# Two graph layers on one core: softmax weights turned by VectorE instead of TensorE, row sums from a column of ones, values evicted whole, and several loads and stores queued elsewhere

## The chip, the cores and the metric

The kernel runs on one core of a Trainium2 chip. The metric is the device time of one execution in microseconds (us), as the median of several runs. Engines are named as in the profile: PE is TensorE, DVE is VectorE, ACT is ScalarE, POOL is GpSimd, and SP is the engine that only issues transfers.

## The reference

Input x has 128 graphs of 64 nodes with 768 features, all float32, and adj is a 0/1 matrix of 64x64 for each graph. Two layers follow each other, both with a residual and a layer norm.

```python
# layer 0, per graph: attention of h with itself, masked and renormalised
p = softmax(h @ h.T / sqrt(768)); delta = p * adj
attn = delta / (delta.sum(2) + 1e-10)
ctx = upper(attn) @ (h @ W_left.T + b_left) + diag(attn) * (h @ W_self.T + b_self) \
    + lower(attn) @ (h @ W_right.T + b_right)
x = layernorm(h + relu(layernorm_affine(ctx)))
# layer 1, per graph: 12 heads of 64
q, k, v = (x @ W + b for W in (Wq, Wk, Wv))          # split into heads
s = where(adj > 0, q @ k.T / 8 + beta * adj, -9e15)
x = layernorm(x + softmax(s) @ v)
```

## The kernel before

**Tiling.** The 8192 tokens are cut into 16 blocks of 512 tokens (8 graphs). A tile of 128 tokens (T = 4 of them in a block) holds two graphs, g = 0 and 1, one in each half of the partitions. Layer 0 of block m = n+1 is worked on beside layer 1 of block n. All arithmetic is float32.

**The big products.** Six weight matrices, s (self), l (left), r (right), v, q and k, are applied by `seven()` with seven products of half size in place of eight (Strassen-like). It runs 14 groups of matmuls, numbered 0 to 13 here: for each of the seven factors in the order 1, 2, 6, 5, 7, 4, 3 one group for j = 0 and one for j = 1. Two PSUM tiles X and two Y (tags "X" and "Y", `ps_st`) take the sums; `first()` copies an intermediate sum out and `last()` writes a result. An accumulation goes on in the same X after `first()` has read it, so the next group that adds to this X waits for that read. For s, l, r and v (`by_tokens`) each group is three products with 384 columns; for q and k (`projected`, one call for each of three head groups hg) it is three with 256 columns, and there `first()` runs on ACT.

**The pieces of the weights.** [...] `prepare()` forms the seven factors at the start and stores those that are new to DRAM; after that every stage streams its seven pieces of 576 KB through the four buffers of `wst`, on SP's queue. The q and k pieces are stored by POOL's queue in `qk_d`.

**The order of work.** From the main loop on, the order is as written. Stages follow each other: `left` (side_part l of block m), `right` (side_part r), `own` (self_part), `val` (values of block n), `qk[0]`, `qk[1]`, `qk[2]` (projected). Hooks are callables that a stage runs before group number `place`; `at(left, 11, sides, m)` puts `sides` before group 11 of `left`. Small work waits in two queues, `urgent` and `lazy`, from which `step()` takes one item after each group; items marked `act` (work for ACT) and GAP let the lazy queue have its turn as well, and `settle(key)` runs everything that a later part needs at once. Hooks of n = 1 to 14 carry layer 1 of the block before, p = n-1.

**Layer 1's attention.** `scores(n, hg)` makes 32 small products into two PSUM tiles, scales and masks them on DVE and queues max, subtraction, exponential (one ACT instruction of 128x1024), sum, reciprocal and multiplication (all 128x1024 on DVE). `turned_weights` turns the result with 8 PE transposes of 128x128 into PSUM tiles `ps_e` and copies them back with two ACT copies to `eT`. `weighted` multiplies with v into `ps_y`, and `added` adds that to x. Head group 0 is scored in `qk[1]` and weighted in `qk[2]`, head group 1 is scored in `qk[2]` and weighted in the next block's `left`, head group 2 is scored and weighted in `left`.

**Values.** Rows of v must lie in the half of the partitions that their product with eT reads, so `last()` in `values` writes each 128x384 result with four DVE instructions of 64x192, which also move between the halves.

**The last block** has nothing beside its layer 1; its attention is done at the end, for two tiles at a time.

Of the kernel before, what the change touches and what calls it, by code (L numbers as in the profile page):

```python
# [11 lines left out]
F32 = mybir.dt.float32  # L12
# [32 lines left out]
def gnn_two_layers(ctx: ExitStack, tc, x, adj, wl, bl, ws, bs, wr, br, gamma, beta,  # L45
# [14 lines left out]
    ps_tr = ctx.enter_context(tc.tile_pool(name="ps_tr", bufs=2, space=PSUM))  # L60
    ps_mm = ctx.enter_context(tc.tile_pool(name="ps_mm", bufs=2, space=PSUM))
# [68 lines left out]
    def settle(key):  # L130

        for queue in (urgent, lazy):
            while any(item[0] == key for item in queue):
                queue.popleft()[1]()
# [3 lines left out]
    pieces = {}  # L138
# [5 lines left out]
    def prepare(nm, quarter_pool, sum_pool, waits=(0, 0, 0)):  # L144

        w = weights[nm].rearrange("(p c) e -> p c e", c=KC)
        src = {(0, 0): w[:, 0:HC, 0:HALF], (0, 1): w[:, 0:HC, HALF:D],
               (1, 0): w[:, HC:KC, 0:HALF], (1, 1): w[:, HC:KC, HALF:D]}  # L150
        b = {}
        for q in ((0, 0), (1, 0), (0, 1), (1, 1)):
            b[q] = quarter_pool.tile([P, HC, HALF], F32, tag="w", name=f"b{q[0]}{q[1]}_{nm}")
            nc.sync.dma_start(out=b[q], in_=src[q])
        t5, t6, t4 = (sum_pool.tile([P, HC, HALF], F32, tag="w", name=f"t{i}_{nm}") for i in (5, 6, 4))
        in_sbuf = {1: b[0, 0], 2: b[1, 0], 3: b[1, 1], 5: t5, 6: t6, 7: b[0, 1], 4: t4}
        key = ("w", nm)
        if nm in "slrv":
            d = tc.dram_tile([4, P, HC, HALF], F32, name=f"d_{nm}")
            pieces[nm] = {1: src[0, 0], 2: src[1, 0], 3: src[1, 1], 5: d[0], 6: d[1], 7: d[2], 4: d[3]}  # L160

        def store(i):
            if nm in "slrv":
                if i in (5, 6, 7, 4):
                    nc.gpsimd.dma_start(out=pieces[nm][i], in_=in_sbuf[i])
            else:

                with tc.issue_after(last_sum[1].ins):
                    for hg in range(NHG):
                        nc.gpsimd.dma_start(out=qk_d[hg, i - 1, :, "qk".index(nm)],  # L170
                                            in_=in_sbuf[i][:, :, hg * P : (hg + 1) * P])

        def formed(i, out, left, right):
            nc.vector.tensor_tensor(out, left, right, ALU.subtract)
            store(i)

        def idle():
            pass

        later(key, *[idle] * waits[0], partial(formed, 5, t5, b[0, 1], b[0, 0]),  # L180
              *[idle] * waits[1], partial(formed, 6, t6, b[1, 1], t5), partial(formed, 7, b[0, 1], b[1, 1], b[0, 1]),
              *[idle] * waits[2], partial(formed, 4, t4, b[1, 0], t6))
        if nm in "qk":
            later(key, lambda: store(1), lambda: store(2), lambda: store(3))
        return in_sbuf

    def transposed(src, xT, t):

        for c0 in range(0, KC, 3):
            ps = ps_tr.tile([P, 4, P], F32, tag="tr", name="ps_x")  # L190
            for c in range(3):
                nc.tensor.transpose(ps[:, c, :], src[:, c0 + c :: KC], ident)
            nc.scalar.copy(xT[:, c0 : c0 + 3, t * P : (t + 1) * P], ps[:, 0:3, :])
# [92 lines left out]
    def by_tokens(nm, S, last, in_sbuf=None, hooks={}):  # L286
# [3 lines left out]
        def factors(i, j):  # L290
            if i not in wt:
                wt[i] = wst.tile([P, HC, HALF], F32, tag="w", name=f"w{nm}")
                nc.sync.dma_start(out=wt[i], in_=pieces[nm][i])
            return [(S[i][:, k, j * P : (j + 1) * P], wt[i][:, k, :]) for k in range(HC)]
# [78 lines left out]
    def sides(n):  # L373
# [3 lines left out]
        aps = ps_tr.tile([P, T, P], F32, tag="tr", name="ps_a")  # L377
# [108 lines left out]
    def values(n, hooks={}):  # L486


        blk = blocks[n]
        v = l1_p.tile([P, T, 2, HP, HD], F32, tag="v", name=f"v_{n}")  # L490
        blk["v"] = v

        def last(t, h, ps, part):
            def pairs(a):
                return a.rearrange("p (j r d) -> p r j d", r=2, d=HD)

            add = pairs(bias["v"][:, h * HALF : (h + 1) * HALF] if part is None else part)
            for r in range(2):
                for g in range(2):
                    rows = slice(g * L, (g + 1) * L)  # L500
                    nc.vector.tensor_tensor(v[r * L : (r + 1) * L, t, g, h * 3 : (h + 1) * 3, :],  # L501
                                            pairs(ps)[rows, r], add[rows, r], ALU.add)

        by_tokens("v", blk["S"], last, None, hooks)
# [30 lines left out]
    def scores(n, hg, pool=None):  # L535

        blk = blocks[n]
        q, k = blk["qk"]

        s = (pool or l1s_p).tile([P, T, 2, 2, L], F32, tag="lr" if pool else "s", name="s")  # L540
# [13 lines left out]
        s8 = s.rearrange("p t c r m -> p (t c r) m")  # L554
        mx = st.tile([P, T * 4], F32, tag="mx1", name="mx1")
        z = st.tile([P, T * 4], F32, tag="z1", name="z1")
        rz = st.tile([P, T * 4], F32, tag="rz1", name="rz1")

        def per_row(v):
            return v[:, :, None].to_broadcast([P, T * 4, L])  # L560

        def sums():
            nc.vector.tensor_reduce(z, s8, AX.X, ALU.add)
            nc.vector.reciprocal(rz, z)

        later(("s", n, hg),
              lambda: nc.vector.tensor_tensor(s4, s4, add[:, :, None, :].to_broadcast([P, T, 4, L]), ALU.add),
              lambda: nc.vector.tensor_reduce(mx, s8, AX.X, ALU.max),
              lambda: nc.vector.tensor_tensor(s8, s8, per_row(mx), ALU.subtract),
              act(lambda: nc.scalar.activation(s8, s8, AF.Exp)), GAP, sums,  # L570
              lambda: nc.vector.tensor_tensor(s8, s8, per_row(rz), ALU.mult), queue=urgent)
        blk[hg] = s

    def turned_weights(n, hg, tiles=range(T), pool=None):

        blk = blocks[n]
        settle(("s", n, hg))
        e = blk[hg]
        if 0 in tiles:
            blk["eT", hg] = (pool or l1_p).tile([P, T, 2, P], F32, tag="lr" if pool else "eT", name="eT")  # L580
        eT = blk["eT", hg]
        for t0 in tiles[::2]:
            ps = ps_tr.tile([P, 4, P], F32, tag="tr", name="ps_e")
            for t in range(2):
                for c in range(2):
                    nc.tensor.transpose(ps[:, 2 * t + c, :], e[:, t0 + t, c].rearrange("p r m -> p (r m)"), ident)  # L586
            nc.scalar.copy(eT[:, t0 : t0 + 2].rearrange("p t c i -> p (t c) i"), ps)

    def weighted(n, hg, tiles=range(T)):

        blk = blocks[n]
        xt, v, eT = blk["x"], blk["v"], blk["eT", hg]
        y = [ps_mm.tile([P, T, 2, HD], F32, tag="mm", name=f"ps_y{r}") for r in range(2)]
        for t in tiles:
            for c in range(2):
                for r in range(2):
                    rows = slice(r * L, (r + 1) * L)
                    for g in range(2):
                        cols = slice(g * L, (g + 1) * L)
                        nc.tensor.matmul(y[r][cols, t, c, :], lhsT=eT[rows, t, c, cols],  # L600
                                         rhs=v[rows, t, g, hg + c * HC, :], start=True, stop=True)

        def added(t):
            res = xt[t].rearrange("p (c k r d) -> p r c k d", c=2, k=HC, r=2)
            for r in range(2):
                nc.vector.tensor_add(res[:, r, :, hg, :], res[:, r, :, hg, :], y[r][:, t])

        def both(ts):
            for t in ts:
                added(t)  # L610

        later(("y", n, hg), *[partial(both, tiles[i : i + 2]) for i in range(0, len(tiles), 2)], queue=urgent)
# [66 lines left out]
    l1s_p = ctx.enter_context(tc.tile_pool(name="l1s", bufs=2))  # L679
# [6 lines left out]
    for n in range(NBLK):  # L686
# [13 lines left out]
        if p >= 0:  # L700
            one, two, three = (left, left, right) if not last else (qk[0], qk[1], qk[1])
            at(one, 1 if not last else 2, scores, p, 2)
            at(one, 1 if not last else 2, turned_weights, p, 1)
            at(one, 5, weighted, p, 1)
            at(two, 11 if not last else 2, turned_weights, p, 2)
# [3 lines left out]
        if not last:  # L709
            if n > 0:  # L710
# [9 lines left out]
                at(right, 9, begin1)  # L720
# [5 lines left out]
                at(own, 0, begin2)  # L726
                for t in range(T):
                    at(own, t, lambda t=t: fetch["fs"][t]())
                for a in range(P // Q):
                    at(right, 9 + a, lambda a=a: sq1["fs"][a]())  # L730
# [48 lines left out]
        if not last:  # L779
            at(qk[2], 2, turned_weights, n, 0)  # L780
# [4 lines left out]
    values(n, {2: [partial(scores, n, 2, l0t)]})  # L785

    for t0 in (0, 2):
        for hg in range(NHG):
            turned_weights(n, hg, range(t0, t0 + 2), l0t if hg else None)
        for hg in range(NHG):  # L790
            weighted(n, hg, range(t0, t0 + 2))
            settle(("y", n, hg))
        finish(n, range(t0, t0 + 2))
# [32 lines left out]
```

## Time and profile before

| | |
|---|---|
| median of 3 runs | 3092.37 us (3086.59 to 3094.2) |
| span of the profiled execution | 3078.1 us |
| PE busy | 2983.9 us, 97% |
| DVE busy | 2227.8 us, 72% |
| ACT busy | 396.8 us, 13% |
| POOL busy | 354.3 us, 12% |
| data moved | 541.20 MB, mean 176 GB/s |

A row of the groups' table reads: line, engine, operation, output<-inputs, shapes, xcount, then busy us and mean ns of one, then idle time of the engine just before and what ended it. A row of the timeline reads: start, duration, engine, line, operation, count, and in brackets how long the engine had been idle and for whom it had waited. One product in float32 shows as two matmul records, so a group of three products is x6.

In the middle of the run the pattern repeats every block: `projected` for head group 0 starts at 1392.4 us in one block and at 1580.5 us in the next, 188.2 us later.

### The profile page before, as it was taken

How to read it: one execution, taken by the hardware profiler on the slowest of the kernel's cores; microseconds unless marked ns; L12 is line 12 of the kernel's file. 1: busy time of each engine (PE TensorE's matmuls, PEld its weight loads, DVE VectorE, ACT ScalarE, POOL GpSimd, SP SyncE). 2: the span in 40 equal slices, each digit the busy share in tenths (PEclk: the TensorE clock that was granted, in tenths of full speed). 3: DMA queues.
4: the chain of work that ended last, by engine and by line, in shares of the span. 5: the costliest groups of instructions: out<-in, count | busy, mean ns of one | idle time of the engine just before them, and what ended most of it. 6: DMA issues, size and time to landing. Idle time of an engine off the chain costs nothing.

```text
span 3078.1 us, 45049 instructions
## 1 busy us (share of the span) xinstructions
PE 2983.9 (97%) x18144; PEld 2015.0 (65%) x18144; DVE 2227.8 (72%) x4163; ACT 396.8 (13%) x691; POOL 354.3 (12%) x317
## 2 busy tenths in 40 slices
PE   8899999999999999999999999999999999999997
PEld 5457657576675766758567585665757667575685
DVE  5758767686776867768687686867768677686756
ACT  0101102021020200202011020110201102020031
POOL 2321010110101101011010111101011010110000
PEclk9999999999999999999999999999999999999998
DMA  8663655737557474574645756456573655746433
GB/s 284 211 230 121 190 174 166 216 118 217 152 161 213 124 229 139 161 215 145 212 139 162 211 160 208 132 179 191 161 221 119 215 156 162 220 127 220 128 123 119
DMA packets 261070, 541.20 MB, mean 176 GB/s; under 512 B 28576, under 2 KB 165408, under 8 KB 260864
## 3 DMA queue, kind: packets, MB, share of 16 engines
q1 hardware_dynamic: 185424, 429.38, 44.1%
q10 hardware_dynamic: 60848, 44.05, 7.2%
q0 software_dynamic: 14592, 64.89, 5.4%
q8 instruction: 145, 2.38, 0.3%
q14 instruction: 61, 0.50, 0.0%
HBM read 473.37 MB, written 64.88 MB: 175 GB/s over the span
## 4 chain that ended last, share of the span: by engine, by line
PE 77%; DVE 7%; issue 7%; DMA 7%; POOL 1%; ACT 0%; ACTq 0%; SPq 0%; POOLq 0%; DVEq 0%
PE ps_X L269 38%; PE ps_Y L269 30%; DMA ws<-in_L_gnn_W_self_dram 6%; DVE v L501 4%; PE ps_ctx L425 3%; DVE hT L211 2%; PE sc L548 1%; PE ps_y L600 1%; PE u L331 1%; PE ps_e L586 1%; DVE u L298 1%; DMA b_l<-in_L_gnn_W_left_dram 1%; DVE stats L239 0%; PE ps_a L379 0%; DMA d_v<-t_v 0%
## 5 line engine op out<-in xcount | busy, mean ns | idle before, releaser
L269 PE MATMUL ps_X<-xT,wqk 128*128 128x256 f32 x1728 | 388.8, 379 | 0.0
L269 PEld LDWEIGHTS ps_X<-xT,wqk 128*128 128x128 f32 x1728 | 328.2, 190 | 48.1 <-issue 0.4
L269 PE MATMUL ps_Y<-S,wqk 128*128 128x256 f32 x1152 | 264.3, 379 | 0.0
L410 DVE TENSOR_TENSOR lr<-ps_Y,u 64x384 f32<-64x384 f32 x384 | 213.2, 555 | 62.6 <-PE ps_Y L269 56.2
L522 ACT ACTIVATE uqk<-ps_X,bq 128x256 f32<-128x256 f32 x144 | 68.2, 474 | 1419.5 <-PE ps_X L269 1419.5
L269 PEld LDWEIGHTS ps_Y<-S,wqk 128*128 128x128 f32 x1152 | 218.9, 190 | 29.8
L269 PE MATMUL ps_X<-wv,xT 128*128 128x384 f32 x576 | 199.2, 492 | 0.3
L239 DVE BATCH_NORM_STATS2 stats<-o 128x6 f32<-128x384 f32 x384 | 192.4, 542 | 1.8
L269 PE MATMUL ps_X<-ws,hT 128*128 128x384 f32 x540 | 181.7, 491 | 7.4 <-DMA ws<-d_s 7.4
L269 PE MATMUL ps_X<-wl,hT 128*128 128x384 f32 x540 | 183.7, 486 | 0.0
L269 PE MATMUL ps_X<-wr,hT 128*128 128x384 f32 x540 | 179.1, 486 | 0.0
L501 DVE TENSOR_TENSOR v<-ps_Y,u 64x192 f32<-64x192 f32 x384 | 136.4, 355 | 41.7 <-PE ps_Y L269 35.6
L269 PE MATMUL ps_Y<-xT,wqk 128*128 128x256 f32 x576 | 138.7, 386 | 27.8 <-DVE v L501 17.9
L269 PEld LDWEIGHTS ps_X<-wv,xT 128*128 128x128 f32 x576 | 106.7, 190 | 85.8 <-issue 9.6
L269 PEld LDWEIGHTS ps_X<-ws,hT 128*128 128x128 f32 x540 | 103.5, 192 | 79.8 <-issue 9.7
L269 PEld LDWEIGHTS ps_X<-wr,hT 128*128 128x128 f32 x540 | 102.5, 190 | 71.3
L269 PEld LDWEIGHTS ps_X<-wl,hT 128*128 128x128 f32 x540 | 100.4, 190 | 61.1
L269 PE MATMUL ps_X<-S,wqk 128*128 128x256 f32 x576 | 138.2, 385 | 0.0
L269 PEld LDWEIGHTS ps_Y<-xT,wqk 128*128 128x128 f32 x576 | 104.3, 190 | 51.6 <-issue 23.8
L298 DVE TENSOR_TENSOR u<-ps_X,bv 128x384 f32<-128x384 f32 x96 | 53.5, 557 | 114.7 <-PE ps_X L269 114.1
L298 DVE TENSOR_TENSOR u<-ps_X,bl 128x384 f32<-128x384 f32 x96 | 53.4, 556 | 112.5 <-PE ps_X L269 110.6
L619 POOL DMA_DIRECT2D out_dram<-o x64 | 34.6, 541 | 862.2 <-DVE o L618 862.0
(183 smaller groups left out, 4715.2 us busy)
## 6 DMA issues: line engine op xcount, KB each, us to landing
wqk<-qk_d SPq DMA_DIRECT2D x336, 384.0 KB, 3.0
wv<-d_v SPq DMA_DIRECT2D x64, 576.0 KB, 4.8
ws<-d_s SPq DMA_DIRECT2D x60, 576.0 KB, 9.0
wl<-d_l SPq DMA_DIRECT2D x60, 576.0 KB, 5.0
wr<-d_r SPq DMA_DIRECT2D x60, 576.0 KB, 3.7
wv<-in_L_gnn_Wv_dram SPq DMA_DIRECT2D x48, 576.0 KB, 4.0
ws<-in_L_gnn_W_self_dram SPq DMA_DIRECT2D x45, 576.0 KB, 7.4
wl<-in_L_gnn_W_left_dram SPq DMA_DIRECT2D x45, 576.0 KB, 4.1
```

Of the source, the lines that this page charges most:

```text
L211: nc.vector.transpose(xT[:, c, :].rearrange("p (s j) -> p s j", j=Q), sq[:, :, c::KC])
L239: nc.vector.bn_stats(stats[:, h, :], tiles[t][:, h * HALF : (h + 1) * HALF])
L269: nc.tensor.matmul(ps, lhsT=a, rhs=b, start=(c == 0 and i in (1, 2, 5)), stop=(c == len(fs) - 1), skip_group_check=True)
L298: nc.vector.tensor_tensor(u, ps, bias[nm][:, b * HALF : (b + 1) * HALF], ALU.add)
L331: nc.tensor.matmul(u[g * L : (g + 1) * L, t, :], lhsT=xT[:, c, tok], rhs=xT[:, c, tok], start=(c == 0), stop=(c == KC - 1))
L410: nc.vector.tensor_tensor(lr[t][half * L : (half + 1) * L, g, cols], ps[rows], bias[nm][rows, cols] if part is None else part[rows], ALU.add)
L425: nc.tensor.matmul(ps[g * L : (g + 1) * L, 0:HALF], lhsT=blk["aT"][:, t, g * L : (g + 1) * L], rhs=blk["lr"][t][:, g, cols], start=True, s ...
L501: nc.vector.tensor_tensor(v[r * L : (r + 1) * L, t, g, h * 3 : (h + 1) * 3, :], pairs(ps)[rows, r], add[rows, r], ALU.add)
L522: nc.scalar.activation(u, ps, AF.Identity, bias=bias["qk"[j]][:, c : c + 1])
L548: nc.tensor.matmul(sc[r][g * L : (g + 1) * L, t, c, :], lhsT=q[rows, c, tok], rhs=k[rows, c, tok], start=True, stop=True)
L586: nc.tensor.transpose(ps[:, 2 * t + c, :], e[:, t0 + t, c].rearrange("p r m -> p (r m)"), ident)
L619: nc.gpsimd.dma_start(out=out_t[n, t], in_=xt[t])
```

## The change

1. **Weights turned by DVE.** The exponential is no longer one ACT instruction: 16 ACT instructions of 32x256 per head group each read a square of 32 rows by 32 columns per (t, c) from s and write it to its mirrored place of eT. Two DVE transposes of 128x512 then turn each square of 32x32 in place. PE's transposes, their PSUM tiles (`ps_tr`) and ACT's copies go, and `ps_mm` gets all four PSUM buffers. s has one buffer, eT two.
2. **Sums by a column of ones.** v gets a 65th column of ones per head, so that the product with unnormalised weights gives the row sum in column 64. The sum, reciprocal and multiplication over 128x1024 go. `added` takes a reciprocal of 128x4 and four multiply-adds of 128x64 for each of four PSUM tiles per head group, in place of 8 additions of 128x128.
3. **Values evicted whole.** One DVE instruction of 128x384 in place of four; afterwards three ACT copies of 64x1536 swap the two blocks that lie in the wrong half (not in the last block, which goes on as before).
4. **Queues.** Loads of Wk wait until block 1's third piece of l has been issued; the stores of q's pieces go to SP's queue, after the last piece of s of block 1, in place of POOL's. In the main loop `begin1` (the reload of layer 0's result, turned) moves from `right` 9 to `left` 10, and the loads of x from `own` 0 to `right` 8.

The diff, cut to its core:

```diff
-    ps_tr = ctx.enter_context(tc.tile_pool(name="ps_tr", bufs=2, space=PSUM))
-    ps_mm = ctx.enter_context(tc.tile_pool(name="ps_mm", bufs=2, space=PSUM))
+    ps_mm = ctx.enter_context(tc.tile_pool(name="ps_mm", bufs=4, space=PSUM))
...
-            nc.sync.dma_start(out=b[q], in_=src[q])
+            with tc.issue_after(streamed["l"][2]) if nm == "k" else ExitStack():
+                nc.sync.dma_start(out=b[q], in_=src[q])
...
-                with tc.issue_after(last_sum[1].ins):
+                queue, first = (nc.sync, streamed["s"][6]) if nm == "q" else (nc.gpsimd, last_sum[1].ins)
+                with tc.issue_after(first):
                     for hg in range(NHG):
...
+            if not in_place:
+                nc.vector.tensor_tensor(v[:, t, :, heads, 0:HD], pairs(ps), add, ALU.add)
+                return
...
+        if not in_place:
+            low, high = v[0:L, :, 1, :, 0:HD], v[L:P, :, 0, :, 0:HD]
+            swap = l0t.tile([P, T, HP, HD], F32, tag="lr", name="swap")
+            later(("v", n), act(lambda: nc.scalar.copy(swap[0:L], high)), act(lambda: nc.scalar.copy(high, low)),
+                  act(lambda: nc.scalar.copy(low, swap[0:L])), queue=urgent)
...
+                    nc.scalar.activation(e[cols, :, rows], pairs[rows, :, cols], AF.Exp)
...
+            nc.vector.transpose(e, e)
...
-              act(lambda: nc.scalar.activation(s8, s8, AF.Exp)), GAP, sums,
-              lambda: nc.vector.tensor_tensor(s8, s8, per_row(rz), ALU.mult), queue=urgent)
+              *[act(partial(exponentials, range(a, a + at_once))) for a in range(0, P // Q, at_once)], GAP,
+              partial(turn, 0), partial(turn, 1), queue=urgent)
...
-                    nc.tensor.transpose(ps[:, 2 * t + c, :], e[:, t0 + t, c].rearrange("p r m -> p (r m)"), ident)
-            nc.scalar.copy(eT[:, t0 : t0 + 2].rearrange("p t c i -> p (t c) i"), ps)
...
-                nc.vector.tensor_add(res[:, r, :, hg, :], res[:, r, :, hg, :], y[r][:, t])
+            nc.vector.reciprocal(rz, ps[:, :, :, HD])
+                    nc.vector.scalar_tensor_tensor(res[:, r, c, hg, :], ps[:, t, c, 0:HD], rz[:, t, c : c + 1],
+                                                   res[:, r, c, hg, :], ALU.mult, ALU.add)
...
-            at(one, 1 if not last else 2, scores, p, 2)
-            at(one, 1 if not last else 2, turned_weights, p, 1)
+            at(one, 1 if not last else 2, scores, p, 2, 1 if last else 2)
             at(one, 5, weighted, p, 1)
-            at(two, 11 if not last else 2, turned_weights, p, 2)
             at(two, 13 if not last else 5, weighted, p, 2)
...
-                at(right, 9, begin1)
+                at(left, 10, begin1)
...
-                at(own, 0, begin2)
+                at(right, 8, begin2)
                 for t in range(T):
-                    at(own, t, lambda t=t: fetch["fs"][t]())
+                    at(right, 8 + t, lambda t=t: fetch["fs"][t]())
                 for a in range(P // Q):
-                    at(right, 9 + a, lambda a=a: sq1["fs"][a]())
+                    at(left, 10 + a, lambda a=a: sq1["fs"][a]())
...
-    values(n, {2: [partial(scores, n, 2, l0t)]})
+    values(n, {6: [partial(scores, n, 2, 2, l0t)]}, True)
```

## The prediction

> **What bounds the kernel now.** I read the page's busy shares and slices first, then the groups with their forms, then the waits, then the timeline of one block of the middle on PE, ACT and DVE, then the first 280 us and the last 220 us.
>
> ```profile
> PE 2983.9 (97%) x18144; PEld 2015.0 (65%) x18144; DVE 2227.8 (72%) x4163; ACT 396.8 (13%) x691; POOL 354.3 (12%) x317
> ...
> PE   8899999999999999999999999999999999999997
> ```
>
> PE works nearly without a gap from the third slice to the second last. Each block needs 4 stages of 42 products of 384 columns at 0.3225 us (an X and Y pair of groups, x12, takes 3.87 us) and 3 of 42 at 0.216 us (x12 in 2.59 us): 54.2 + 27.2 = 81.4 us per pass of the records, and as every product has two records, 162.8 us of the 188.2 us of a block. Only the other 25 us can shrink: small products, PE's transposes, and waits. So a DVE or ACT instruction more or less matters only where PE stands waiting for it.
>
> ```profile
> 1459.09 1.16 PE L548 MATMUL sc<-k,q 64*64 64x64 f32 x64
> 1460.18 1.09 PE L586 MATMUL ps_e<-ident,s 128*128 128x128 f32 x8
> 1461.11 2.10 PE L269 MATMUL ps_X<-wl,hT 128*128 128x384 f32 x6
> ...
> 1483.08 0.66 PE L379 MATMUL ps_a<-ident,a 128*128 128x128 f32 x4 [0.29 <-ACT eT L587]
> ...
> 1487.55 1.16 PE L600 MATMUL ps_y<-v,eT 64*64 64x64 f32 x64
> ...
> 1523.35 4.11 PE L269 MATMUL ps_Y<-ws,hT 128*128 128x384 f32 x12 [1.55 <-DMA ws<-in_L_gnn_W_self_dram]
> ...
> 1583.99 1.53 PE L269 MATMUL ps_Y<-xT,wqk 128*128 128x256 f32 x6 [0.71 <-PE ps_X L269]
> 1586.80 1.53 PE L269 MATMUL ps_Y<-xT,wqk 128*128 128x256 f32 x6 [1.28 <-DVE v L501]
> ```
>
> Here the reader sees what is to be had: a turn of weights stands on PE for 0.93 us (1460.18 to 1461.11); `ps_a` waits 0.29 us for an ACT copy; the second piece of `ws` is late by 1.55 us; the first Y groups of `qk[0]` wait 1.99 us. The 0.71 us is named after PE, but DVE's last-but-one `v` eviction ended at 1583.9, so both are DVE's backlog of v. The list of waits has the same over the run:
>
> ```profile
> PE ps_Y L269 <- DMA ws<-in_L_gnn_W_self_dram: 21.3, 13, 3.8
> ...
> PE ps_Y L269 <- DVE v L501: 17.9, 14, 1.3
> ...
> PE ps_Y L269 <- PE ps_X L269: 9.8, 14, 0.7
> ...
> PE ps_X L269 <- DMA ws<-d_s: 7.4, 1, 7.4
> ```
>
> **What the Trainium skill says.** "ScalarE: Activation LUTs", What ACT_TABLE_LOAD costs: an activation with immediate scale and bias takes 186 ns + 0.833 ns per element, and ones back to back overlap by 93 ns. The trace agrees: 128x256 took 417 ns (skill: 399). "VectorE: DVE Perf Modes", The three transpose paths: DVE turns only squares of 32x32, which is why ACT must place the squares. And its TRN2 errata section: an fp32 tensor_tensor takes (N+151)/0.96 ns, nearly all fixed for small N; 128x128 here took 279 ns (skill: 291). "Trainium Kernel Development and Optimization", Key Constraints: transfers from SP, ACT and POOL run on the same 16 DMA engines, so another queue changes only the order; here the late `ws` piece shares the engines with ACT's and SP's loads of x.
>
> **The change part by part.**
>
> *PE's transposes.* 48 turns (384 records of 8). 45 of them, outside the last block, cost 0.93 us each on PE's path: -41.9 us. The wait of `ps_a` for ACT's copy goes with them: -4.1 us. 65 columns for 64 in `weighted` add under 2% of 1.1 us, 0.02 us each: nothing. I can't bound from the trace what an odd count or rows of 260 bytes cost.
>
> *Values.* A group of v costs DVE 1.46 us now and will cost 0.56 us (a full eviction of 128x384, L392). With `u` 0.56 and a transpose of hT 1.09, a group of `val` then needs 2.2 us at most, against 1.94 us of PE, and only 2 groups do; so the backlog is gone when `qk[0]` wants Y: -27.7 us (17.9 + 9.8). The three swap copies take ACT an estimated 186 + 0.833 x 1536 = 1.47 us each. They sit before the second `uqk` of `qk[0]`, which then comes about 2 us late; its Y is read a group later and X is needed three groups later, so it is hidden.
>
> *Exponentials on ACT.* One 128x1024 of 1.06 us and two copies (1.07 us) become 16 of 32x256. No row has that form; nearest is 128x256 at 417 ns, and with overlap 310 ns. I take 0.31, so 5 us per head group; the other end is 0.47 (a `uqk`), 7.5 us. The waiter is `first()` in `projected`, behind them in ACT's queue. In `qk[1]` the first 8 can start at 1425.86 (the old exponential's start) and end 2.5 to 3.8 us later, and the next `uqk` is due at 1429.25, with 1.3 us until PE adds to its X: hidden at both ends. The others delay only the last evictions of X by 1 to 3 us, and the next stage wants those X's 3 groups later. Hidden.
>
> *DVE's work.* Per head group two transposes of 1.09 us (L211's form) replace 1.21 + 0.25 + 1.22 us. `added` goes from 1.66 us to 4 x (0.17 + 4 x 0.15 to 0.22), 3.1 to 4.2 us (priced by the skill's 224 ns for 64 elements, less the 0.07 us by which L606's overlap). With v's saving DVE is at or below its 72%: no cost by itself.
>
> *The new wait.* In `left` the second half of head group 2's turn is queued after group 12, and `weighted` stands on PE before group 13. The built order on DVE is: the two lr of group 11, turn 0, the two lr of group 12, turn 1. Durations are from these rows:
>
> ```profile
> 1483.13 1.12 DVE L410 TENSOR_TENSOR lr<-ps_X,bl 64x384 f32<-64x384 f32 x2
> 1484.28 0.69 DVE L381 TENSOR_TENSOR aT<-ps_a,side 128x512 f32<-128x512 f32 x1
> 1485.72 1.12 DVE L410 TENSOR_TENSOR lr<-ps_X,bl 64x384 f32<-64x384 f32 x2 [0.74 <-PE ps_X L269]
> 1487.65 1.12 DVE L410 TENSOR_TENSOR lr<-ps_Y,u 64x384 f32<-64x384 f32 x2 [0.81 <-PE ps_Y L269]
> ```
>
> Group 12 ends on PE at 1487.55. The lr of group 11 end at 1486.84; turn 0 ends at 1487.93; lr of group 12 at 1489.05; turn 1 at 1490.14. The second half of `weighted` (0.55 us) starts then, and so group 13 starts at 1490.7 to 1490.8 in place of 1488.64: 2.2 us of stall (2.1 to 2.7, the upper end if the first half waits for both turns). It comes 14 times: +31 us. In `qk[2]` and at `left` 5 the turns are done 2 us and more before the product, so these don't wait.
>
> *Moved loads.* The four reloads of layer 0's result go at about 1480 in place of 1504, those of x at 1491 to 1498 in place of 1503 to 1510. Around 1480 to 1500 the engines move some 120 to 125 GB/s, and at 1510 to 1530 they move 333 to 366. Adding 1.5 MB to each of two stretches of 10 us gives about 280, under the 390 to 399 reached at the start, so `ws` should be in time and `wr`, loaded four pieces ahead, stay so: 12 waits, 21.3 less the 3.8 of the start, -17.5 us.
>
> *Start.* Block 1's `ws` stage now waits 7.45 + 3.84 us for pieces stuck behind b_k's loads, and two groups then run at a granted clock of 0.51 to 0.67, 1.9 us longer each: 15 us. With b_k and q's stores behind them this goes. But wl's pieces now alternate with 21 stores on SP, some 12.5 MB until the last b_k, at 390 GB/s 32 us after 136 us: b_k lands near 170. DVE's t_k stands ahead of an eviction of `wl` group 9 due near 167, and PE then waits some 4 us; and wl may slip 3 us. Net -8 us (-15 to +5).
>
> *End.* The last block's xT copies on ACT come behind 8 to 12 exponentials: +2 us. After the last product, six `added` at 0.85 to 1.0 us per half take the place of three at 0.88: 2.5 to 3.4 us more per half, less the two last turns and ACT copies (about 1.9 and 3.4 us): +3 us. Together +5 (+2 to +8).
>
> Sum: -41.9 - 4.1 - 27.7 + 31 - 17.5 - 8 + 5 = -63 us, and 3092.4 - 63 = 3029 us, 2% faster.
>
> **The rivals.** *Loads only move their collision:* `wr` or `wl` late in place of `ws`, and nothing won at the start, since the bytes are the same and the start runs at the ceiling. Then 17.5 and 8 us are missing: 3055 us. For it: 13 MB with 35 us to go at the start; against: the valley of 120 GB/s in the middle. *The new wait is hidden,* for instance because DVE reaches turn 1 earlier than these rows say, and the start wins its 15 us: 3029 - 31 - 7 = 2991 us. Against: turn 1 can't precede lr of group 12, which waits for PE. *ACT becomes the bound of the q and k stages:* if small activations across quarters of the partitions cost 0.75 us, 8 of them take 6 us, the `uqk` due at 1429.25 comes at 1432 and PE waits 2 us; later evictions of X make it some 3.6 us in `qk[1]`, 5 in `qk[2]` and 3 in `left`, 11 us x 15 blocks = 165 us: 3190 us, slower. For it: no row shows the form; against: 128x256 at 417 ns.
>
> **How the numbers follow.** Forecast 0.60; collision moved 0.20; wait hidden 0.12; ACT the bound 0.07; the last 0.01 lies near no change. The time is the first's, 3029. The range runs from 2991, the hidden wait, to 3066, which takes in the moved collision (3055) with the upper ends of the new wait (+7) and of the end (+3). Faster by over 0.3% holds in the first three, less something for costs in `weighted` that I can't see: 0.89; same 0.03; slower 0.08.
>
> **What would show it.** Right: no `ps_e` group; the wait of ps_Y for v near 0; a wait of `ps_y`'s load or product for DVE's transpose of eT, 14 times of 2.1 to 2.7 us, as the largest new one; `ws` waits gone; a block near 184 us; the 32x256 activation at 0.40 to 0.42 us. Wrong: waits of PE for ACT's uqk, waits for `wr` or `wl`, or `weighted` longer than 1.2 us without a wait.

## The result and the profile after

The changed kernel takes 2993.76 us (median of 4 runs, 2992.76 to 2993.9), against 3089.48 us before in the same session (3083.96 to 3094.2): ratio 0.969, 95% interval 0.9671 to 0.9709. It is 95.7 us faster; the forecast was 63. The profiled spans differ by less, 3078.1 and 2992.2 us.

The page of the changed kernel, busy time and two rows of the slices:

```profile
PE 2927.3 (98%) x17760; PEld 1981.9 (66%) x17760; DVE 2158.1 (72%) x4331; ACT 677.8 (23%) x1360; POOL 339.0 (11%) x297
...
PE   8999999999999999999999999999999999999996
...
ACT  0103214031140412304032140321404113040342
```

PE is still the bound, ACT's share went from 13 to 23%, DVE's stayed. The list of waits (us in total, times, longest), PE's rows:

```profile
PE ps_y L609 <- DVE eT L585: 17.1, 14, 1.2
...
PE ps_X L272 <- DVE u L301: 6.6, 3, 3.0
PE ps_x L195 <- DMA xa<-in_x_dram: 6.4, 3, 5.2
PE ps_y L609 <- DVE rz L615: 6.3, 5, 4.1
PE ps_ctx L428 <- DVE lr L413: 4.1, 1, 4.1
PE ps_X L272 <- ACT uqk L533: 3.4, 1, 3.4
...
PE ps_x L195 <- ACT xT L196: 2.0, 1, 2.0
```

The rows of before for `ws`, `v` and `ps_a` are gone. One wait comes 14 times, the one that was forecast. The others belong to the start or the end.

The starts of the `sc` products (head group 0, blocks 0 and 14) cut the two profiles into three parts:

| part | before | after | change |
|---|---|---|---|
| up to the first `sc` | 285.26 us | 271.89 us | -13.4 |
| 14 blocks between | 2630.54 us | 2548.53 us | -82.0 |
| from block 14's first `sc` to the end | 162.30 us | 171.78 us | +9.5 |

A block of the middle takes 182.26 us in place of 188.23 (mean of 13 blocks). Side by side, PE's timelines of one block differ in these places only, each read from start to start: from `qk[0]`'s first X group to its `u` products 5.27 us in place of 7.74; the `ws` X group to its Y group 3.86 in place of 5.58, and 0.07 less in this Y group; turn and `ps_a` in `left` 0.44 in place of 1.83; the turns after the other two `sc` 0.83 less each (0.93 up to the next group, which gives 0.10 back); 0.24 less in the last groups of `val`; and group 13 of `left`, later by 1.64 us. The sum is 5.91 us, and these two blocks are 188.17 and 182.26 us long. Here is the last, on PE:

```profile
1427.21 2.10 PE L272 MATMUL ps_X<-wl,hT 128*128 128x384 f32 x6
1429.15 2.10 PE L272 MATMUL ps_Y<-wl,S 128*128 128x384 f32 x6
1431.36 0.70 PE L609 MATMUL ps_y<-v,eT 64*64 64x65 f32 x32
1433.28 0.70 PE L609 MATMUL ps_y<-v,eT 64*64 64x65 f32 x32 [1.22 <-DVE eT L585]
1433.91 2.20 PE L272 MATMUL ps_Y<-wl,S 128*128 128x384 f32 x6
```

From one Y group to the next it is 4.76 us, where the kernel before had 3.12 (1485.52 to 1488.64). DVE's timeline at the same time shows who holds it:

```profile
1428.68 0.69 DVE L384 TENSOR_TENSOR aT<-ps_a,side 128x512 f32<-128x512 f32 x1
1429.35 1.12 DVE L413 TENSOR_TENSOR lr<-ps_X,bl 64x384 f32<-64x384 f32 x2
1430.50 0.71 DVE L585 STREAM_TRANSPOSE eT<-eT 128x512 f32<-128x512 f32 x1
1431.28 1.12 DVE L413 TENSOR_TENSOR lr<-ps_Y,u 64x384 f32<-64x384 f32 x2
1432.42 0.71 DVE L585 STREAM_TRANSPOSE eT<-eT 128x512 f32<-128x512 f32 x1
```

The order is the forecast one (lr of group 11, turn 0, lr of group 12, turn 1), but a turn takes 0.71 us and not 1.09. So turn 0 is over (1431.21) before PE's group 12 is (1431.25), and only turn 1 still stands between the lr of group 12 and the product.

### The profile page after: what moved, and what is told of

Its sections match the earlier page's. It is cut to its first block, busy times and chain, and to the rows that moved or that the text cites. A ratio compares the mean times of both kernels' runs of the same rounds, so it can differ in the third digit from the quotient of the medians.

```text
span 2992.2 us, 45095 instructions
## 1 busy us (share of the span) xinstructions
PE 2927.3 (98%) x17760; PEld 1981.9 (66%) x17760; DVE 2158.1 (72%) x4331; ACT 677.8 (23%) x1360; POOL 339.0 (11%) x297
## 3 DMA queue, kind: packets, MB, share of 16 engines
q10 hardware_dynamic: 60848, 44.05, 8.1%
## 4 chain that ended last, share of the span: by engine, by line
PE 88%; issue 7%; DVE 3%; DMA 1%; POOL 1%; POOLq 0%; ACTq 0%; SPq 0%; DVEq 0%
PE ps_X L272 46%; PE ps_Y L272 35%; PE ps_ctx L428 3%; PE sc L563 2%; PE u L334 1%; PE ps_y L609 1%; DVE lr L413 1%; DVE eT L585 0%; DMA d_v<-t_v 0%; DMA b_s<-in_L_gnn_W_self_dram 0%; DMA b_k<-in_L_gnn_Wk_dram 0%; DVE o L438 0%; PE ps_a L382 0%; DVE t_s L177 0%; DMA bk<-in_L_gnn_bk_dram 0%
## 5 line engine op out<-in xcount | busy, mean ns | idle before, releaser
L581 ACT ACTIVATE eT<-s 32x256 f32<-32x256 f32 x768 | 317.7, 414 | 149.8 <-DVE s L590 139.7
L619 DVE SCALAR_TENSOR_TENSOR o<-ps_y,rz,o 128x64 f32<-128x64 f32 x768 | 165.0, 278 | 6.8
L541 DVE TENSOR_TENSOR q<-ps_Y,uqk 128x256 f32<-128x256 f32 x144 | 60.1, 418 | 112.4 <-ACT uqk L533 59.8
L272 PE MATMUL ps_Y<-wv,S 128*128 128x384 f32 x384 | 133.2, 490 | 0.0
```

Of the source, the lines that this page charges most:

```text
L272: nc.tensor.matmul(ps, lhsT=a, rhs=b, start=(c == 0 and i in (1, 2, 5)), stop=(c == len(fs) - 1), skip_group_check=True)
L541: nc.vector.tensor_tensor(dst, ps, part, ALU.add)
L581: nc.scalar.activation(e[cols, :, rows], pairs[rows, :, cols], AF.Exp)
L619: nc.vector.scalar_tensor_tensor(res[:, r, c, hg, :], ps[:, t, c, 0:HD], rz[:, t, c : c + 1], res[:, r, c, hg, :], ALU.mult, ALU.add)
```

## The experiments

Theory: the change is a sum of four nearly independent gains (loads in the loop, queues at the start, values, softmax), less one new wait, and the forecast had the parts right and some sizes wrong. Rivals: the parts hide each other, so that they don't add up; the loads only move their collision; or ACT was close to becoming the bound.

**Loads of the loop alone**, on the kernel before:

```diff
-                at(right, 9, begin1)
+                at(left, 10, begin1)
...
-                at(own, 0, begin2)
+                at(right, 8, begin2)
```

> The kernel before, with nothing changed but the two loads in the main loop (begin1 at left 10, loads of x at right 8). My theory: the late piece of ws shares the engines with these loads, so the 12 waits of the middle go, 17.5 us by the profile of before. As the timed runs of before lie 6 to 16 us above its profiled one and those of the changed kernel within 1.2 us of each other, I also expect the spread to go and the gain in the timed median to be about 28 us: some 3062. Rival: the collision only moves to wr or wl: within 5 us of before, with waits of PE for wr or wl of 1 us and more in each block. A second rival: the late ws comes from the loop being slower for another reason, and the waits stay.

Measured: 3051.03 us against 3086.01, ratio 0.9887 (0.9873 to 0.99): 35.0 us less, more than either theory had. Every block takes 186.37 us, and the waits for `ws` outside the start are gone; no wait for `wr` or `wl` of any size takes their place. So the collision did not move.

**Queues of the start alone**, on the kernel before:

```diff
+            with tc.issue_after(streamed["l"][2]) if nm == "k" else ExitStack():
+                nc.sync.dma_start(out=b[q], in_=src[q])
...
+                queue, first = (nc.sync, streamed["s"][6]) if nm == "q" else (nc.gpsimd, last_sum[1].ins)
```

> The kernel before, with nothing changed but the queues of the start (loads of Wk behind block 1's third piece of l, stores of q's pieces on SP's queue). Theory: the first scores come 13 us earlier, as in the changed kernel (271.89 against 285.26 us), and this is all: 13 us less, 3076. My prediction had 8. Rival: a part of the 13 us belongs to the other edits (values whole takes 2.5 us out of block 0's qk[0]): 9 to 11 us less.

Measured: 3077.55 us, ratio 0.9978 (0.9967 to 0.9988): 8.5 us less. The first `sc` comes at 276.77 us, 8.5 us earlier. (The profiles of kernels whose loads and stores of the start are as before have it between 281.09 and 286.01 us, so this is good to a few us.) The rival is right: a rest of the 13.4 us belongs to other edits.

**Values alone**, on the kernel before:

```diff
+            if not in_place:
+                nc.vector.tensor_tensor(v[:, t, :, h * 3 : (h + 1) * 3, :], pairs(ps), add, ALU.add)
+                return
...
+            later(("v", n), act(lambda: nc.scalar.copy(swap[0:L], high)), act(lambda: nc.scalar.copy(high, low)),
+                  act(lambda: nc.scalar.copy(low, swap[0:L])), queue=urgent)
```

> The kernel before, with values evicted whole and swapped by three ACT copies, and nothing else changed. Theory: DVE's backlog of v is all that holds PE at the first Y groups of qk[0], so these 2.7 us (start of qk[0] to its u products: 7.74 us before, 5.03 without waiting) go 14 times and once at the start: about 38 us less, 3051. My prediction had 27.7 us. Rival: the three copies of 1.47 us on ACT delay uqk in qk[0], and PE waits there: 15 to 25 us less, with waits of PE for ACT.

Measured: 3049.73 us, ratio 0.9885 (0.9872 to 0.9899): 36.3 us less. PE waits neither for `v` nor for ACT's `uqk`. One wait grew, from 21.3 us in 13 times before:

```profile
PE ps_Y L269 <- DMA ws<-in_L_gnn_W_self_dram: 33.0, 15, 3.9
```

In the profile a block takes 186.77 us, 1.46 less than before: the values give 2.70 (the next experiment), and the grown wait takes the rest back.

**The three together**, that is, the changed kernel without its softmax part (the edits above, all on the kernel before):

> The changed kernel without its softmax part: the kernel before with both queue changes and values evicted whole, and with PE's turns of the weights, its sums and its products as before. Theory: in the steady block the turns and the wait behind them give 2.8 + 0.5 us and cost 1.64 us, so this block is some 183.7 us against 182.26, and at the end it is 5 us shorter: 14 us slower than the changed kernel, about 80 us faster than before (3006 if before is 3086). It gains more than the sum of the three parts measured alone (35.0 + 8.5 + 36.3 = 79.8 us) by the wait for ws that grew in the run with values alone, from 21.3 to 33.0 us, so 80 to 90. Rival: the softmax part is worth the 46 us of PE time that it takes away less 23: 20 to 25 us slower than the changed kernel.

Measured: 3007.51 us against 3086.99, ratio 0.9743 (0.9728 to 0.9758): 79.5 us less, where the parts alone add up to 79.8. A block takes 183.67 us: 188.23 less 1.86 for the loads (the first experiment) and less 2.70 for the values (2.47 and 0.24 in the comparison of the blocks). So the parts add up; that they would gain more together, by the wait that grew in the run with values alone, was not seen. What is left of the change for the softmax is 16.2 us; the medians of this run and of the changed kernel, from two sessions, are 13.8 us apart. The profiles give 16.4 us: 19.65 in the 14 blocks (1.40 each) and 3.79 at the start, less 7.04 at the end. What makes the 3.79 us is not shown.

**The product later**, on the changed kernel:

```diff
-            at(two, 13 if not last else 5, weighted, p, 2)
-            at(three, 0 if not last else 6, finish, p)
+            at(right if not last else two, 1 if not last else 5, weighted, p, 2)
+            at(three, 2 if not last else 6, finish, p)
```

> The changed kernel, with the weighted product of head group 2 moved from before group 13 of left to before group 1 of right, and finish to group 2. Theory: the only new wait of the steady block is this product's wait for DVE's second turn, 1.64 us 14 times, and it is hidden two groups later: 23 us less than the changed kernel, 2971, a block of 180.6 us. Rival: DVE is late as a whole there, so the additions and the norm pushed later hold PE in right or own (bias evictions late): 0 to 10 us less, or a wait of ps_X or ps_Y for DVE in right.

Measured: 2973.06 us against 3086.01, ratio 0.9633 (0.962 to 0.9646). This beats both kernels: its interval lies below that of the changed kernel. PE at the product's new place:

```profile
1425.91 2.10 PE L272 MATMUL ps_X<-wr,hT 128*128 128x384 f32 x6
1427.94 1.16 PE L609 MATMUL ps_y<-v,eT 64*64 64x65 f32 x64
1429.03 2.20 PE L272 MATMUL ps_X<-wr,hT 128*128 128x384 f32 x6
```

The product follows without a wait. A block takes 180.90 us, 1.36 less; of the 1.64 us, 0.28 came back in `right`, where four X groups take 8.18 us in place of 7.90, with the additions now ahead of a `u` in DVE's queue.

**Every exponential twice**, on the changed kernel:

```diff
-                    nc.scalar.activation(e[cols, :, rows], pairs[rows, :, cols], AF.Exp)
+                    for _ in range(2):
+                        nc.scalar.activation(e[cols, :, rows], pairs[rows, :, cols], AF.Exp)
```

> The changed kernel with every exponential issued twice, the second over the first, so that a head group's 16 take 13.6 us of ACT in place of 6.8. Theory: ACT has almost no room in qk[1]: the first 8 end at 1558.20 and uqk starts 0.03 us later, and PE can wait about 1 us for it; with 3.4 us more PE waits 2 to 3 us for uqk in qk[1], and about as much for the weights of head group 1 at left 5, 14 times: 50 to 100 us slower than the changed kernel. Rival: with 23% busy ACT has room for 6.8 us more per head group: within 10 us of the changed kernel.

Measured: 3224.58 us, ratio 1.0449 (1.0428 to 1.047): 231 us slower than the changed kernel, more than twice what I expected. The timeline of ACT in `qk[1]`, then PE's:

```profile
1455.47 0.47 ACT L533 ACTIVATE uqk<-ps_X,bk 128x256 f32<-128x256 f32 x1 [0.82 <-PE ps_X L272]
1455.96 6.97 ACT L582 ACTIVATE eT<-s 32x256 f32<-32x256 f32 x16
1462.96 0.47 ACT L533 ACTIVATE uqk<-ps_X,bq 128x256 f32<-128x256 f32 x1
```

```profile
1457.86 2.75 PE L272 MATMUL ps_X<-xT,wqk 128*128 128x256 f32 x12
1463.49 4.54 PE L272 MATMUL ps_X<-xT,wqk 128*128 128x256 f32 x12 [2.87 <-ACT uqk L533]
```

The wait of 2.87 us in `qk[1]` is as expected; what I had missed are waits for the weights of head group 2 at group 13 of `left` (56.7 us in 28 times, where the changed kernel has 17.1 in 14; at `left` 5, where I had looked for head group 1, there is none), for `q` and `k`, which ACT also evicts at the end of `qk[2]` just before `scores` wants them, and for `u`. An engine at 23% was within a few us of being the bound, because its work comes in the stretch in which PE also waits for its evictions.

**Loads of the loop back**, on the changed kernel:

```diff
-                at(left, 10, begin1)
+                at(right, 9, begin1)
...
-                at(right, 8, begin2)
+                at(own, 0, begin2)
```

> The changed kernel with its two loads of the main loop back at their places of before (begin1 at right 9, x at own 0). Theory: the wait for ws comes back, 1.9 us or more in each of 14 blocks, more since the block is shorter (2.2 us on average in the run with values alone): 26 to 33 us slower than the changed kernel, and a wider spread. Rival: the stall before group 13 of left gives the queue a lead, and less than 10 us comes back.

Measured: 3033.3 us against 3086.99, ratio 0.9825 (0.9808 to 0.9841), 39.5 us slower than the changed kernel. The gain of the loads is there in both kernels, but in this one the wait has another face:

```profile
DVE xT L214 <- DMA sq<-x1d: 70.0, 11, 8.0
...
PE ps_X L272 <- DVE u L301: 30.6, 24, 3.0
```

DVE's transposes of the reloaded tile stand in its queue until the data are there, and the bias evictions `u` behind them make PE wait. The trace names DVE; the cause is the reload.

**Each load alone**, on the kernel before: the diff of the first experiment, with its first pair of lines only, or its second only.

> The kernel before, with the reload of layer 0's result alone moved (begin1 at left 10, on ACT's queue); the loads of x stay at own 0. Theory: two batches of loads beside pieces of ws are too much, one is not; with either moved the wait for ws mostly goes: 25 to 35 us less than before, as with both moved (35). Rival A: the loads of x are the ones that stand ahead of ws, on SP's own queue, so that moving the reload gives less than 10 us. Rival B: the reload is the only cause, 35 us, and moving x alone gives nothing.

> The kernel before, with the loads of x alone moved (begin2 at right 8, SP's queue); the reload stays at right 9. Theory: 25 to 35 us less than before. Rival A (x stands ahead of ws in SP's queue): about 35 us less, all of the gain. Rival B (the reload is the only cause): within 8 us of before, or slower, as both batches now start together at right 8 and 9.

Measured: the reload alone 3052.34 us against 3087.0, ratio 0.9884 (0.9866 to 0.9902), 34.7 us less, as much as both. The loads of x alone 3076.35 us, ratio 0.9959 (0.9943 to 0.9975), 10.7 us less, though its profile still has 20.5 us of waits for `ws` and a block of 187.96 us; where those 10.7 us come from stays open. Of the rivals B is right on the reload, not on x. Why the reload and not x, shows in the transfers. The pieces of `ws` (KB each, median us from issue to landing), before, with x alone moved, and with the reload alone moved:

```profile
ws<-in_L_gnn_W_self_dram SPq DMA_DIRECT2D x45, 576.0 KB, 7.4
...
ws<-in_L_gnn_W_self_dram SPq DMA_DIRECT2D x45, 576.0 KB, 10.8
...
ws<-in_L_gnn_W_self_dram SPq DMA_DIRECT2D x45, 576.0 KB, 4.1
```

And in the busy times by stretches of 10 us (after the engines' columns: PE clock, share of the DMA engines, GB/s; a packet counts where it starts, so that a share can exceed 1). Before, with the reload issued from 1503.82 on:

```profile
1495.00:1505.00 10.00, 10.00 (x33) 5.89 (x32) 8.52 (x21) 0.21 (x1) 0.00 (x0) 1.00 0.48 145
1505.00:1515.00 10.00, 10.00 (x33) 5.89 (x32) 6.45 (x11) 0.00 (x0) 1.08 (x2) 1.00 1.09 280
1515.00:1525.00 10.00, 8.45 (x27) 4.72 (x26) 5.16 (x10) 0.00 (x0) 1.08 (x2) 1.00 1.05 379
```

With the reload alone moved (three of its four pieces issued from 1466.74 on):

```profile
1465.00:1475.00 10.00, 9.71 (x99) 6.28 (x98) 6.21 (x15) 2.36 (x3) 0.00 (x0) 1.00 0.98 211
...
1495.00:1505.00 10.00, 10.00 (x33) 5.89 (x32) 8.34 (x15) 0.00 (x0) 2.07 (x4) 1.00 0.95 346
```

With much of the reload under way the DMA engines are full at 211 to 280 GB/s; without it they move 346 at a share of 0.95. The queues of before from 1505 to 1510 (packets, MB, share of the 16 engines) name the dear bytes:

```profile
q10 hardware_dynamic: 873, 0.66, 70.2%
q1 hardware_dynamic: 366, 0.71, 36.9%
```

ACT's queue (q10), which then holds the reload, takes twice as much of the engines for a MB as SP's (q1), with packets of some 0.75 KB against 1.9 KB. Over the whole run, by the page of before, ACT's queue moves 44.05 MB for 7.2% of the engines and SP's 429.38 MB for 44.1%, 1.6 times as much for a MB; half of ACT's bytes are the reload, the other half x in the same layout. That the packets' size is the reason is likely, but no run varies it. In its new place the reload slows pieces of `wr` (5.9 us to landing for the two issued between 1465 and 1475, where the median is 3.7), and PE does not wait for them.

**Prices.** The changed kernel, in one run, followed by single instructions on idle engines:

```diff
+        nc.vector.transpose(a[:, 0:512], a[:, 0:512])
+        nc.vector.transpose(a[:, 512:1024], a[:, 0:512])
+        nc.vector.transpose(a[:, 512:1024], b[:, 0::KC])
+        nc.vector.transpose(a[:, 0:2048], a[:, 0:2048])
...
+            nc.scalar.activation(e8[r * Q : (r + 1) * Q, :, 0:Q], s8[0:Q, :, r * Q : (r + 1) * Q], AF.Exp)
+        nc.scalar.activation(b[0:Q, 0:256], a[0:Q, 2048:2304], AF.Exp)
+        nc.scalar.activation(b[:, 0:256], a[:, 2048:2304], AF.Exp)
```

> The changed kernel followed by single instructions on idle engines, for their durations alone: DVE transposes of 128x512 in place, into another place, and from a source with a stride of 6 elements, and of 128x2048 in place; on ACT 8 exponentials of 32x256 from quarter to quarter as in the kernel, 8 within one quarter on dense rows, 8 of 128x256 and 8 of 128x1024. Theory: what made me take 1.09 us for a turn is the stride of the source: 0.70 us in place and out of place, 1.08 us with the stride. Rival: writing in place makes it cheap, and out of place takes 1.08. For ACT: the start-to-start interval of 0.425 us belongs to the instruction, not to the strides or quarters: the same 0.41 to 0.43 us in all of 256 elements; rival: dense rows or one quarter come every 0.31 us.

The timeline, in the order of the diff (start, sum of the group, count at the end):

```profile
2994.07 2.89 DVE L811 STREAM_TRANSPOSE probe<-probe 128x512 f32<-128x512 f32 x4
2997.00 2.95 DVE L813 STREAM_TRANSPOSE probe<-probe 128x512 f32<-128x512 f32 x4
2999.99 4.42 DVE L815 STREAM_TRANSPOSE probe<-probe 128x512 f32<-128x512 f32 x4
3004.44 9.35 DVE L817 STREAM_TRANSPOSE probe<-probe 128x2048 f32<-128x2048 f32 x4
...
3005.80 3.45 ACT L821 ACTIVATE probe<-probe 32x256 f32<-32x256 f32 x8
3009.26 3.54 ACT L823 ACTIVATE probe<-probe 32x256 f32<-32x256 f32 x8
3012.83 3.55 ACT L825 ACTIVATE probe<-probe 128x256 f32<-128x256 f32 x8
```

In place a transpose takes 712 ns, out of place 711, with the stride of 6 in the source 1078 (medians of one). So it is the stride. On ACT 8 in a row take 3.45 to 3.55 us in all three forms, 0.43 to 0.45 from start to start: quarters and strides are free, and these exponentials do not overlap.

## Why the prediction was right, and where its sizes were off

Direction and mechanism were right in all parts, and the time lies in the range, 3 us above its lower end. The sum was 33 us short of the change, and that the time still lies in the range is luck in part: its lower end was put there for a hidden wait, which did not come. By its own terms, with the measured size beside each:

| term | forecast | measured | from |
|---|---|---|---|
| loads of the loop | -17.5 | -35.0 | run with loads alone |
| values (backlog of v) | -27.7 | -36.3 | run with values alone |
| start | -8 | -8.5 | run with the start's queues alone |
| softmax: turns, `ps_a`, new wait, end | -10 | -16.2 | change less the three together (13.8 by the two medians) |

*The loads* are the term that failed most, half of the shortfall. Three things were wrong in it. First, I summed idle times from the list of waits; read from start to start the same wait is 1.72 us, not 1.55, and by the steady blocks (188.23 less 186.37) 1.86 us, 26 us in 14 blocks. Secondly, I took one profile for all runs: its span of 3078.1 us is below nearly every timed run of before (medians 3086 to 3089 us), and I infer, without a trace of those runs, that the rest of the 35 us are longer waits of the same kind in them; the runs without this wait, of the changed kernel, lie within 1.2 us. Thirdly, the cause was half right: I counted GB/s and named ACT's and SP's loads together. Moving the reload alone gives the whole gain, and the share of the DMA engines, 1.09 in the windows of before at 280 GB/s, would have told that they were full.

*The values* had the mechanism right and the size read in the same too narrow way: 1.99 us of idle time in the list are 2.47 us from start to start, with 0.24 us more in `val`: 2.7 us, 14 times 38. In the run with values alone the wait for `ws`, grown by 11.7 us, takes some of it back. The three copies are hidden, as forecast: the run with values alone has no wait for ACT in `qk[0]`.

*The new wait* came where, when and as often as forecast. Its size of 2.2 us was 1.64, 23 us in place of 31, because I priced a turn by the kernel's other transposes, 1.09 us, whose source has a stride of 6; these have none. With 0.71 us for a turn, turn 0 hides behind PE's group 12 as well. The Trainium skill points to the lower price: "Vector Engine (DVE) Microarchitecture Reference", section The reshape front-end and per-opcode configuration, says of the transpose that it is "pipelined to sustain one element per cycle per lane". The runs agree on an even pace for a dense source: from 512 to 2048 elements a transpose grows from 712 to 2312 ns, 1.04 ns per element. With the stride it is slower, 1078 ns for 512.

*The turns* gave nearly what was forecast: two of a block 0.83 us each in place of 0.93, as the group behind gives 0.10 back, and the third, with the wait of `ps_a`, 1.39 in place of 1.22.

*The end* was forecast at +5 (+2 to +8) and took +9.5 in the profiles. The +2 for the xT copies is there (27.41 us between two `sc`, 26.38 before, which still had a turn), the tail from the `sc` of `qk[2]` on is 4.8 us longer, and two turns fewer between give back 1.7. Missed were 5.35 us in block 14's `qk[1]`:

```profile
2828.78 1.69 ACT L581 ACTIVATE eT<-s 32x256 f32<-32x256 f32 x4
2830.48 1.28 ACT L250 ACT_TABLE_LOAD   x1
2831.77 0.21 ACT L250 ACTIVATE std<-std 128x4 f32<-128x4 f32 x1
2832.00 1.28 ACT L581 ACT_TABLE_LOAD   x1
2833.29 1.69 ACT L581 ACTIVATE eT<-s 32x256 f32<-32x256 f32 x4
2835.01 0.47 ACT L533 ACTIVATE uqk<-ps_X,bq 128x256 f32<-128x256 f32 x1
```

In this block a norm's square root falls between two pieces of the exponential, with two table loads, and `uqk` comes so late that PE waits 3.40 us.

*Exponentials hidden*: right, but with less room than I wrote. The interval is 0.425 us and not 0.31, so that the first 8 end 0.03 us before their `uqk` starts, just when it is due. At twice the exponentials the loss is 231 us; the rival that made ACT the bound at 0.75 us each had put 165 us on the forecast, so its working was of the right order. It fell only by the price.

*The rivals*: the collision did not move (first experiment). The wait was not hidden; that rival's time of 2991 us was met by other terms, for which it had no reason.

## What to carry to other kernels

Price a wait from start to start against an undisturbed block, and not by the idle time in the list of waits, which was a tenth to a quarter too small here; and don't take one profile for the median where the wait is one for a DMA. For a collision of transfers read the share of the DMA engines, not GB/s, and ask which queue's packets are the dear ones. An instruction in an in-order queue that waits for late data stops all behind it, so the page names the wrong engine; and work moved to an idle engine is free only in the stretch where nobody waits for that engine, which one run with the work doubled tells.

## What the runs showed of the hardware

- Exponentials in a row did not overlap: 8 of 32x256 in 3.45 us, 8 of 128x256 in 3.55 us, at durations of 414 to 416 ns. The prediction took 93 ns of overlap from the Trainium skill, "ScalarE: Activation LUTs", What ACT_TABLE_LOAD costs. Other activations of these runs do overlap by about that much, as a square root and a copy of the kernel before, 0.09 us (below). For these exponentials the measurement decides; what sets the two kinds apart is not shown.
- A 32-partition activation cost as much as a 128-partition one, 414 and 416 ns, and from any quarter to any quarter the kernel's took 398 to 419 ns.
- A DVE transpose of 128x512 float32 took 0.71 us dense and 1.08 us from a source with a stride of 6 elements.
- The 16 DMA engines were full at 280 GB/s in one stretch of 10 us (share 1.09) and at 379 in the next (1.05). In the first half of the first, ACT's queue had 70% of them for 0.66 MB.

The two overlapping activations, on ACT:

```profile
1440.16 0.20 ACT L247 ACTIVATE std<-std 128x4 f32<-128x4 f32 x1
1440.27 1.05 ACT L587 COPY eT<-ps_e 128x512 f32<-128x512 f32 x2
```
